# A two-layer graph attention kernel: table products of the first layer issued in fours on four PSUM banks, and the second layer's queries made inside the second layer

## The chip, the cores and the metric

The kernel runs on one core of a Trainium2 chip. The metric is device time in microseconds (us) for one launch, from the host's side of the program to its end; a profiled execution of the same program gives the span from its first to its last instruction and the time of every instruction.

## What is computed

A graph of 6250 nodes (128 features) and 200,000 edges goes through two layers of typed multi-head attention (8 heads of 16). Cut to what matters:

```python
def typed_linear(x, t, W):                 # one of 16 matrices per node, by its type
    y_all = jnp.einsum('nd,tdo->nto', x, W)
    return jnp.take_along_axis(y_all, t[:, None, None], axis=1)[:, 0]

def gt_layer(x, ntype, etype, src, dst, Wk, Wq, Wv, Wa, Watt, Wmsg, pri, skip, g, b):
    k, q, v = (typed_linear(x, ntype, W).reshape(n, 8, 16) for W in (Wk, Wq, Wv))
    kT = jnp.einsum('nhd,htdo->nhto', k, Watt)      # 32 edge types: the "table"
    vT = jnp.einsum('nhd,htdo->nhto', v, Wmsg)
    a = jnp.einsum('ehd,ehd->eh', kT[src, :, etype], q[dst]) * pri[:, etype].T / 4.0
    hag = segment_sum(vT[src, :, etype] * edge_softmax(a, dst, n)[:, :, None], dst)
    h = silu(typed_linear(hag, ntype, Wa))
    h = h * alpha + x * (1.0 - alpha)               # alpha = sigmoid(skip[ntype])
    return layernorm(h) * g + b

out = layernorm(x + (gt_layer(gt_layer(x)) @ ff_w + ff_b))
```

## The kernel before

Nodes are put in order of their degree and cut into 49 tiles of 128. A table in device memory holds, for every node and each of 32 edge types, 256 numbers (the products kT and vT). A preparation stage sorts, makes the first layer's table and lasts to about 0.8 ms. Then two layers follow one another.

In a layer GpSimd (POOL) issues 1613 gathers (`gather`, L887): each is an indirect DMA that brings one edge of each of 128 nodes from the table into a ring in SBUF (64 slots in the first layer, 96 in the second). VectorE (DVE) attends over the ring (`attend`: products at L908, sums at L910, weighting at L935, sums at L939); a tile has 61 edges at first and 23 at the end. Tiles are taken in 15 groups (`LAST`: ten of 4 tiles, then 3, 2, 2, 1, 1, numbered from 0). When a group's attention is done, `behind` applies the typed matrix Wa: transposes on TensorE (PE), 16 masks on DVE (`typed_cols`, L1010: the columns of nodes of one type), 16 matmuls on PE (L1018), then activation, skip and norm.

In the first layer `project` follows: it stores h (`hid`), runs 16 more masks and 3 x 16 matmuls with the second layer's Wk, Wv and Wq into the banks ak, av and aq, and turns the third product into rows that it stores as `qrows`. `next_tables` then makes the second layer's table, tile by tile: `table_rows` issues 16 matmuls a tile (L472) of 32 rows by 512 columns, two half-tiles of 8, which ScalarE (ACT) or DVE copy from PSUM into one of two staging buffers st (L481); `scatter` (L1130) sends each half with one indirect DMA of 2 MB issued by POOL, between the gathers. All of a group's steps in the first layer hold one lane (banks xb, aq, av; a lock), so that groups follow one another there. The first layer's own queries (`first_rows`) use the lane too. The second layer loads its queries from `qrows`. It cannot begin before the last scatter has landed, since it gathers from that table.

The order on each engine is written down by a planner (`Plan`): threads yield an engine, a duration and the times that they need; the planner takes the one that can start first (a rank breaks ties) and emits its instructions. Each engine runs its instructions in this order, whatever the real times are. A scatter is placed on POOL 8 us (`MARGIN`) after the planned end of its half's copies; in the last two groups without that margin.

In `table_rows` the number of banks decides the form, and a matmul that is planned alone is taken to use a quarter of PE:

```python
quad = rows if len(banks) >= rows else 1          # rows = 4
us = yield "PE", Work(TAB, QUAD if quad > 1 else width / P), [*needs, *emptied[-len(banks):][:quad]]
```

Of the kernel before, what the change touches and what calls it, by code (L numbers as in the profile page):

```python
# [31 lines left out]
F32 = mybir.dt.float32  # L32
# [27 lines left out]
XML = (4, 16)  # L60
# [6 lines left out]
RANK = dict(table=0, empty=0, gather=1, attend=1.6, prepare=2, mask=3, typed=3, late=4, query=1, behind=1.2, masks=1.4)  # L67
# [164 lines left out]
def gnn_kernel(ctx: ExitStack, tc: tile.TileContext, x, src, dst, etype, ntype, Wk, Wq, Wv, Wa,  # L232
# [636 lines left out]
    tabs, ak, av, aq = [bank(ps, f"tab{i}") for i in range(3)], bank(ps, "ak"), bank(ps, "av"), bank(ps, "aq")  # L869
# [13 lines left out]
    wq0 = []  # L883
# [62 lines left out]
    def query_rows(fp, n0, q):  # L946

        xo = fp.tile([P, GT, P], F32, tag="xs", name="xs", bufs=XS[0])
        nc.sync.dma_start(out=xo[:, 0], in_=xperm[ds(n0, P)])
        kinds = fp.tile([P, GT * P], F32, tag="types", name="types", bufs=XS[0])  # L950
        nc.sync.dma_start(out=kinds[:, :P], in_=tyrow[ds(n0, P)][None, :].to_broadcast([P, P]))
        nc.tensor.transpose(xb[:, :P], xo[:, 0], ident)
        for t in range(NT):
            xm = fp.tile([P, GT * P], F32, tag="xm", name="xm", bufs=XML[0])
            nc.vector.scalar_tensor_tensor(xm[:, :P], kinds[:, :P], float(t), xb[:, :P], op0=ALU.is_equal, op1=ALU.mult)
            nc.tensor.matmul(aq[:, :P], wq0[0][:, t], xm[:, :P], start=(t == 0), stop=(t == NT - 1))
        qT = fp.tile([P, GT * P], F32, tag="yT", name="yT")
        nc.vector.tensor_copy(qT[:, :P], aq[:, :P])
        nc.tensor.transpose(xb[:, :P], qT[:, :P], ident)
        nc.vector.tensor_copy(q, xb[:, :P])  # L960

    def attend_over(fp, layer, ring):
# [3 lines left out]
        with tc.For_i(0, rounds, 1):  # L966
            nc.sync.dma_start(out=over.rearrange("(t p) c -> p t c", p=P), in_=low)
            with tc.For_i(0, NP, P) as n0:
# [17 lines left out]
                if layer:  # L986
                    nc.sync.dma_start(out=q, in_=qrows[ds(n0, P)])
                else:
                    query_rows(fp, n0, q)
# [11 lines left out]
    def typed_cols(fp, xm_bufs, xT, types, M, maps, needs):  # L1001
# [11 lines left out]
        plan.spawn(mask(), RANK["masks"])  # L1013
# [43 lines left out]
    def behind(fp, layer, i, hag, fetched, needs, weights, wa, at):  # L1057
# [5 lines left out]
        xb, aq, av, lock = lane  # L1063
# [4 lines left out]
        us = yield from typed_cols(fp, XML[layer], xT, types, M, [(wa, aq)], [us, got])  # L1068
        yT, us = yield from copied4(fp, "yT", aq, M, [us], 1 + layer)
# [22 lines left out]
    def project(fp, i, h, types, weights, needs, at):  # L1092
# [44 lines left out]
    def head(fp, i, h, lane, needs, at):  # L1137
        xb, _, av, lock = lane
# [7 lines left out]
        for j in range(n):  # L1146
            nc.tensor.matmul(av[:, j * P : (j + 1) * P], oT[:, j * P : (j + 1) * P], fw, start=True, stop=True)
# [4 lines left out]
        nc.vector.tensor_tensor(o, av.rearrange("p (j m) -> p j m", j=GT)[:, :n],  # L1152
# [42 lines left out]
    def attends(fp, layer, ring, pieces, st, weights, wa, landed, freed):  # L1195
# [22 lines left out]
        def first_rows(i):  # L1218

            n = len(LAST[i])  # L1220
            turn = lanes[0][3].take()
# [3 lines left out]
            us = yield from typed_cols(fp, XML[layer], xT, types, n * P, [(wq0[0], aq)], [us])  # L1225
            qT, us = yield from copied4(fp, "yT", aq, n * P, [us])
# [5 lines left out]
            lanes[0][3].give(e[0])  # L1232
            rows[i] = q, e[0]
            asked[i].us = e[0]

        def load_rows(i):
            if layer:
                us = yield "SP", 0.4, ()
                rows[i] = load4(fp, "qr", qrows, LAST[i][0], len(LAST[i]), 2), us + 3.0
            else:  # L1240
                yield "SP", 0.0, [asked[i]]
# [7 lines left out]
        if not layer:  # L1249
            plan.spawn(first_rows(0), RANK["behind"])  # L1250
            plan.spawn(first_rows(1), RANK["behind"])
# [30 lines left out]
    for layer in range(L):  # L1282
        last = layer == L - 1
        with tc.tile_pool(name=f"wp{layer}", bufs=1) as wp, tc.tile_pool(name=f"fp{layer}", bufs=1) as fp, \
                tc.tile_pool(name=f"ring{layer}", bufs=1, side="right") as rp:
            locks = {"s": Lock()}
            lanes = [(xb, aq, av, Lock()), (xb, aq, av, Lock()), (*tabs, Lock())]
# [3 lines left out]
            if not last:  # L1291
                wq0.append(load_typed(wp, "wq0", Wq[0]))
# [141 lines left out]
```

## Time and profile before

| | us |
|---|---|
| three runs: median (lowest to highest) | 5501.67 (5501.55 to 5515.91) |
| the profiled execution's own time | 5500.28 |
| its span, first to last instruction | 5498.5 |
| first gather of the first layer | 802.1 |
| last gather of the first layer | 3138.98 |
| first gather of the second layer | 3288.00 |

The span falls into preparation, first layer, a stretch without gathers between the layers, and the second layer. In both layers the share of busy time is less telling than what POOL does from one gather to the next.

### The profile page before, as it was taken

The page shows a single profiled execution, that of the slowest core. Times are in us where ns is not written, and L with a number is a line of the kernel's source. Part 1 is how long each engine was busy: PE and PEld are TensorE (multiplying, and loading weights), DVE is VectorE, ACT ScalarE, POOL GpSimd, SP SyncE. Part 2 cuts the span into 40 slices and gives each one's busy share as a digit, 9 for nine tenths or more (in the row PEclk, how much of TensorE's full clock was granted, in tenths as well). Part 3 has the DMA queues.
Part 4 walks back from the last instruction along what each step waited for, and adds up shares of the span by engine and source line. Part 5 has one row for each costly group of instructions (what it writes and reads, how often), then busy time and mean ns, then how long its engine had stood idle before and what let it go on. Part 6 is the DMA issues. An engine that isn't in the chain of part 4 may idle for free. (4 is left out here: it accounts for less than half of the span.)

```text
span 5498.5 us, 34997 instructions
## 1 busy us (share of the span) xinstructions
PE 2728.7 (50%) x8557; PEld 1359.0 (25%) x8557; DVE 3741.5 (68%) x5254; ACT 953.7 (17%) x1840; POOL 3554.6 (65%) x3543
## 2 busy tenths in 40 slices
PE   6889962276677677878789870011011101111112
PEld 4555531032233233333334440000000000000002
DVE  5786746777678777767766624666676667767677
ACT  2233420021222222222223330000000000000001
POOL 0403317777777777777766417777777777777775
PEclk8899986577677677867778775555555555555556
DMA  7669883354645655565555443333333333333332
GB/s 248 261 250 399 353 320 103 106 168 158 222 160 170 220 195 168 189 215 198 189 169 206 172 159 107 102 110 109 99 108 108 109 100 108 108 110 108 104 109 77
DMA packets 315967, 917.37 MB, mean 167 GB/s; under 512 B 82465, under 2 KB 163613, under 8 KB 278121
## 3 DMA queue, kind: packets, MB, share of 16 engines
q0 software_dynamic: 176864, 645.82, 36.6%
q1 hardware_dynamic: 138888, 269.24, 13.4%
q8 instruction: 68, 1.11, 0.1%
q14 instruction: 147, 1.20, 0.1%
HBM read 482.08 MB, written 432.74 MB: 166 GB/s over the span
## 5 line engine op out<-in xcount | busy, mean ns | idle before, releaser
L887 POOL DMA_INDIRECT ring<-table,idx_all x3226 | 3242.7, 1005 | 1203.0 <-issue 961.3
L908 DVE TENSOR_TENSOR ring<-ring,sb 128x2048 f32<-128x2048 f32 (+13 forms) x261 | 453.8, 1739 | 783.8 <-DMA ring<-table,idx_all 773.0
L481 ACT COPY st<-tab 128x512 f32<-128x512 f32 x1207 | 651.9, 592 | 954.4 <-PE tab L472 713.3
L939 DVE TENSOR_REDUCE add<-ring 128x128 f32<-128x2048 f32 (+13 forms) x269 | 732.6, 2724 | 7.5
L472 PE MATMUL tab<-bk,kT 32*128 32x512 f32 x1568 | 612.3, 805 | 182.2 <-ACT st L481 177.4
L1010 DVE SCALAR_TENSOR_TENSOR xm<-types,xb 128x512 f32<-128x512 f32 (+3 forms) x848 | 469.8, 586 | 323.4 <-PE aq L1018 291.1
L472 PE MATMUL tab<-bv,vT 32*128 32x512 f32 x1568 | 558.7, 801 | 7.0 <-ACT st L481 6.5
L1018 PE MATMUL aq<-xm,wq 128*128 128x512 f32 (+3 forms) x960 | 453.8, 589 | 93.1 <-DVE xm L1010 93.1
L910 DVE TENSOR_REDUCE sb<-ring 128x128 f32<-128x2048 f32 (+13 forms) x269 | 473.0, 1758 | 7.1
L935 DVE TENSOR_TENSOR ring<-ring,sb 128x2048 f32<-128x2048 f32 (+13 forms) x269 | 469.4, 1745 | 0.0
L1018 PE MATMUL aq<-xm,wa 128*128 128x512 f32 (+3 forms) x736 | 332.7, 608 | 151.9 <-DVE xm L1010 151.3
L1172 ACT COPY sb<-qr 128x128 f32<-128x128 f32 x96 | 25.9, 270 | 1986.0 <-DVE sb L910 1789.5
L411 PE MATMUL xb<-ident,hag 128*128 128x128 f32 x75 | 25.4, 416 | 672.1 <-DVE hag L1278 669.3
L481 DVE COPY st<-tab 128x512 f32<-128x512 f32 x361 | 234.6, 686 | 156.9 <-PE tab L472 121.3
L439 PE MATMUL kv<-xm,wk 128*128 128x256 f32 (+1 forms) x800 | 262.9, 412 | 57.2 <-DVE xm L424 57.1
L472 PEld LDWEIGHTS tab<-bk,kT 32*128 32x128 f32 x1568 | 187.8, 225 | 399.0 <-ACT st L481 316.4
L1018 PEld LDWEIGHTS aq<-xm,wq 128*128 128x128 f32 x960 | 194.3, 219 | 332.4 <-issue 184.8
L1130 POOL DMA_INDIRECT table<-st,half x98 | 98.7, 1007 | 253.1 <-ACT st L481 213.2
L439 PE MATMUL kv<-xm,wv 128*128 128x256 f32 (+1 forms) x800 | 246.5, 391 | 0.0
L1018 PE MATMUL ak<-xm,wk 128*128 128x512 f32 (+3 forms) x480 | 226.2, 555 | 22.3 <-DVE xm L1010 22.2
L1018 PEld LDWEIGHTS aq<-xm,wa 128*128 128x128 f32 x736 | 152.2, 226 | 341.4 <-DVE xm L1010 205.4
L472 PEld LDWEIGHTS tab<-bv,vT 32*128 32x128 f32 x1568 | 189.5, 222 | 189.4 <-ACT st L481 133.3
(198 smaller groups left out, 2710.3 us busy)
## 6 DMA issues: line engine op xcount, KB each, us to landing
table<-st SPq DMA_DIRECT2D x196, 1024.0 KB
ring<-table,idx_all POOLq DMA_INDIRECT x3226, 2.8
state<-init SPq DMA_DIRECT2D x2, 3528.0 KB
state<-state SPq DMA_DIRECT2D x98, 72.0 KB
types<-tyrow SPq DMA_DIRECT2D x20, 256.0 KB
rows<-in_x_dram SPq DMA_DIRECT2D x24, 128.0 KB
types_i<-in_node_type_dram SPq DMA_DIRECT2D x24, 128.0 KB
xperm<-xg SPq DMA_DIRECT2D x12, 256.0 KB
```

The source lines that it names most:

```text
L439: nc.tensor.matmul(to, w[:, t], xm, start=False, stop=last_of)
L472: nc.tensor.matmul(tab, cT[here, nodes], blk[here, t0 : t0 + per].rearrange("p t o -> p (t o)"), start=True, stop=True)
L481: (nc.scalar.copy if e == "ACT" else nc.vector.tensor_copy)(to, tab.rearrange("p (t o) -> p t o", o=width))
L887: nc.gpsimd.indirect_dma_start(out=ring[:, place], out_offset=None, in_=tables[layer], in_offset=bass.IndirectOffsetOnAxis(ap=idx[:, s : s ...
L908: nc.vector.tensor_tensor(kk, kk, q[:, None, :].to_broadcast([P, m, P]), op=ALU.mult)
L910: nc.vector.tensor_reduce(sc[:, s0 : s0 + m], kk.rearrange("p s (h d) -> p s h d", h=H), axis=AX.X, op=ALU.add)
L935: nc.vector.tensor_tensor(vv.rearrange("p s (h d) -> p s h d", h=H), vv.rearrange("p s (h d) -> p s h d", h=H), sc[:, s0 : s0 + m, :, None ...
L939: nc.vector.tensor_reduce(add, vv.rearrange("p s c -> p c s"), axis=AX.X, op=ALU.add)
L1010: nc.vector.scalar_tensor_tensor(xm[:, :M], types[:, :M], float(t), xT[:, :M], op0=ALU.is_equal, op1=ALU.mult)
L1018: nc.tensor.matmul(to[:, :M], w[:, t], xm[:, :M], start=(t == 0), stop=(t == NT - 1))
L1130: s = nc.gpsimd.indirect_dma_start(out=tables[1].rearrange("(n t) c -> n (t c)", t=RT // 2), out_offset=bass.IndirectOffsetOnAxis(ap=half[ ...
L1172: nc.scalar.copy(q, rows[0][:, j])
```

## The change

The first layer's table products get a fourth bank, and so are issued in fours (one matmul for each 32-row strip, on four banks). The bank comes from aq: the lane's typed products, the first layer's queries and the project step now share av. `project` makes queries (Wq) only for groups 0 and 1, after keys and values are copied out; for groups 2 to 14 a new background thread of the second layer, `early_rows`, loads h and types, makes the masks and the 16 matmuls on two of the four table banks, and stores `qrows`. The second layer's mask buffers go from 16 to 8, and it loads Wq at its start. A loop for nodes of higher degree, which is skipped with this data, makes its queries itself in both layers.

```diff
-XML = (4, 16)
+XML = (4, 8)
-RANK = dict(table=0, ..., behind=1.2, masks=1.4)
+RANK = dict(table=0, ..., behind=1.2, masks=1.4, early=1.8)
-    tabs, ak, av, aq = [bank(ps, f"tab{i}") for i in range(3)], bank(ps, "ak"), bank(ps, "av"), bank(ps, "aq")
+    tabs, ak, av = [bank(ps, f"tab{i}") for i in range(4)], bank(ps, "ak"), bank(ps, "av")
...
     def project(fp, i, h, types, weights, needs, at):
...
-        end = yield from typed_cols(fp, XML[0], xT, types, M, [(wk, ak), (wv, av), (wq, aq)], [us])
-        at["ty"][i].us = end
+        end = yield from typed_cols(fp, XML[0], xT, types, M, [(wk, ak), (wv, av)], [us])
+        if i > 1:
+            at["ty"][i].us = end
...
         plan.spawn(next_tables(i, kT, vT, bk, bv, max(ks, vs), at), RANK["table"])
-        qT, us = yield from copied4(fp, "yT", aq, M, [end])
-        us = yield from turned(xb, qT, n, [us])
-        q, qs = yield from copied4(fp, "q", xb, M, [us])
-        lanes[0][3].give(qs)
-        yield "SP", 0.4, [qs]
-        nc.sync.dma_start(out=qrows[t0 * P : t0 * P + M].rearrange("(j p) d -> p j d", p=P),
-                          in_=q.rearrange("p (j d) -> p j d", d=P)[:, :n])
+        us = max(ks, vs)
+        if i < 2:
+            us = yield from typed_cols(fp, XML[0], xT, types, M, [(wq, av)], [us])
+            at["ty"][i].us = us
+            qT, us = yield from copied4(fp, "yT", av, M, [us])
+            us = yield from turned(xb, qT, n, [us])
+            q, us = yield from copied4(fp, "q", xb, M, [us])
+            got = yield "SP", 0.4, [us]
+            nc.sync.dma_start(out=qrows[t0 * P : t0 * P + M].rearrange("(j p) d -> p j d", p=P),
+                              in_=q.rearrange("p (j d) -> p j d", d=P)[:, :n])
+        lanes[0][2].give(us)
...
+        def early_rows():
+            xb, acc, _ = lanes[3]
+            free, sent = [0.0, 0.0], [0.0, 0.0]
+            for i, g in list(enumerate(LAST))[2:]:
+                n = len(g)
+                got = yield "SP", 0.9, [free[-2]]
+                xs = load4(fp, "xq", hid, g[0], n, 1)
+                types = fp.tile([P, GT * P], F32, tag="tq", name="tq", bufs=2)
+                nc.sync.dma_start(out=types[:, : n * P], in_=tyrow[...][None, :].to_broadcast([P, n * P]))
+                xT, us = yield from transposed(xb, xs, n, [got + 3.0])
+                us = yield from typed_cols(fp, XML[layer], xT, types, n * P, [(wqs[layer], acc)], [us], "early")
+                free.append(us)
+                qT, us = yield from copied4(fp, "qT", acc, n * P, [us])
+                us = yield from turned(xb, qT, n, [us])
+                q, us = yield from copied4(fp, "q", xb, n * P, [us, sent[-1]])
+                us = yield "SP", 0.4, [us]
+                nc.sync.dma_start(out=qrows[...], in_=q...)
+                sent.append(us + 2.5)
+                asked[i].us = us + 2.5
...
-            lanes = [(xb, aq, av, Lock()), (xb, aq, av, Lock()), (*tabs, Lock())]
+            lanes = [(xb, av, Lock()), (xb, av, Lock()), (*tabs[:2], Lock()), (*tabs[2:], Lock())]
...
+            wqs.append(load_typed(wp, "wq0", Wq[layer]))
```

Since the planner works with other durations, the order changes on every engine. Three places matter below.

On POOL, at the first group's scatters in the first layer (L887 is a gather, L1130 before and L1132 after is a scatter of half a tile), before:

```order
L887 DMA ring<-table_60,idx_all 128x256 x287
L1130 DMA table_61<-st_5708,half 12544x4096
L887 DMA ring<-table_60,idx_all 128x256 x4
L1130 DMA table_61<-st_5709,half 12544x4096
L887 DMA ring<-table_60,idx_all 128x256 x13
```

and now:

```order
L887 DMA ring<-table_60,idx_all 128x256 x275
L1132 DMA table_61<-st_5708,half 12544x4096
L887 DMA ring<-table_60,idx_all 128x256 x5
L1132 DMA table_61<-st_5709,half 12544x4096
L887 DMA ring<-table_60,idx_all 128x256 x12
```

The first scatter stands 12 gathers earlier than before; the distance from one tile's scatters to the next tile's hardly changes (4 and 13 gathers, now 5 and 12). Counted through the layer, a four-tile group's first scatter stood 86 to 97 gathers behind the group's own last gather and now stands 77 to 87 behind it. Nine scatters stand behind the last gather of the layer (ten before).

On PE, near the end of the first layer, where group 13 (one tile) applies Wa (`wa`) while the tables of group 12 are made (`tab`), before:

```order
L1018 MATMUL aq<-xm,wa 128x128 x3
L472 MATMUL tab_5444<-bv,vT 128x512
L1018 MATMUL aq<-xm,wa 128x128 x2
L472 MATMUL tab_5445<-bv,vT 128x512
L1018 MATMUL aq<-xm,wa 128x128
L472 MATMUL tab_5446<-bk,kT 128x512
```

and now:

```order
L411 MATMUL xb<-ident,hag 128x128
L1015 MATMUL av<-xm,wa 128x128 x10
L472 MATMUL tab_5444<-bv,vT 128x512
L472 MATMUL tab_5445<-bv,vT 128x512
L472 MATMUL tab_5446<-bv,vT 128x512
L472 MATMUL tab_5447<-bv,vT 128x512
L1015 MATMUL av<-xm,wa 128x128 x6
```

Table matmuls stood one by one among others and now stand four together.

On DVE, at the end of the attention over the layer's last tile (tile 48; L1278 before and L1304 after is its last instruction, `xm 128x128` are the masks of group 13's step with Wa), before:

```order
L942 TENSOR_TENSOR hag<-hag,add 128x128
L1276 TENSOR_SCALAR den<-den 128x8
L1277 RECIPROCAL den<-den 128x8
L1278 TENSOR_TENSOR hag<-hag,den 128x128
L1027 COPY q<-xb 128x256
L1010 SCALAR_TENSOR_TENSOR xm<-types,xb 128x128 x16
```

and now:

```order
L919 TENSOR_TENSOR sb<-sb,top 128x192
L1007 SCALAR_TENSOR_TENSOR xm<-types,xb 128x128 x14
L924 TENSOR_REDUCE den<-sb 128x8
L925 TENSOR_TENSOR state<-state,sb 128x8
L926 TENSOR_TENSOR den<-den,state 128x8
L927 TENSOR_TENSOR hag<-state,sb 128x128
L1007 SCALAR_TENSOR_TENSOR xm<-types,xb 128x128 x2
L935 TENSOR_TENSOR ring<-ring,sb 128x10x128
```

Group 13's masks stood behind the last tile's attention and now stand inside it.

## Rows read from the trace of the kernel before

**Rows 1.** The page, part 1: busy time by engine over the span.

```profile
PE 2728.7 (50%) x8557; PEld 1359.0 (25%) x8557; DVE 3741.5 (68%) x5254; ACT 953.7 (17%) x1840; POOL 3554.6 (65%) x3543
```

**Rows 2.** Stretch; its us; PE, PEld, DVE, ACT, POOL busy; PEclk; DMA; GB/s.

```profile
802.00:1200.00 398.00, 139.43 (x308) 61.92 (x308) 266.55 (x281) 25.46 (x51) 296.21 (x296) 0.64 0.44 121
1200.00:2400.00 1200.00, 875.41 (x1936) 377.10 (x1934) 882.76 (x1065) 283.13 (x542) 918.95 (x914) 0.71 0.57 191
2400.00:2815.00 415.00, 327.90 (x728) 141.92 (x728) 312.88 (x418) 103.64 (x202) 305.42 (x304) 0.71 0.58 195
2815.00:3139.00 324.00, 302.54 (x777) 137.30 (x775) 200.67 (x327) 88.76 (x173) 188.30 (x189) 0.77 0.50 175
3139.00:3288.00 149.00, 127.27 (x518) 76.64 (x518) 54.17 (x141) 53.67 (x101) 10.71 (x12) 0.77 0.38 155
3288.00:5448.00 2160.00, 255.01 (x644) 132.32 (x644) 1448.45 (x1778) 127.58 (x246) 1658.02 (x1649) 0.54 0.37 107
```

**Rows 3.** POOL's waits, 802 to 2400 us: total, times, longest.

```profile
POOL ring L887 <- DVE add L939: 12.7, 3, 12.1
POOL table L1130 <- ACT st L481: 4.1, 4, 3.2
```

**Rows 4.** POOL's waits, 2400 to 3139 us.

```profile
POOL table L1130 <- ACT st L481: 100.0, 20, 15.8
```

**Rows 5.** PE's timeline, 3204 to 3226 us: start, length, instruction, count.

```profile
3206.98 1.12 PE L472 MATMUL tab<-bk,kT 32*128 32x512 f32 x2
3208.03 0.49 PE L1018 MATMUL ak<-xm,wk 128*128 128x128 f32 x2
```

**Rows 6.** Groups of instructions by line, 815 to 3290 us.

```profile
L472 PE MATMUL tab<-bk,kT 32*128 32x512 f32 x784 | 487.5, 957 | 178.6 <-ACT st L481 177.4
L472 PE MATMUL tab<-bv,vT 32*128 32x512 f32 x784 | 419.6, 958 | 4.3 <-ACT st L481 4.2
L481 ACT COPY st<-tab 128x512 f32<-128x512 f32 x766 | 416.6, 591 | 630.7 <-PE tab L472 417.6 <-DMA table<-st,half 211.0
L1018 PE MATMUL aq<-xm,wq 128*128 128x512 f32 x640 | 350.5, 662 | 90.5 <-DVE xm L1010 90.5
```

**Rows 7.** PE's timeline in the preparation: matmuls of the first table.

```profile
180.69 2.45 PE L472 MATMUL tab<-bv,vT 32*128 32x512 f32 x8
...
500.79 1.14 PE L472 MATMUL tab<-bv,vT 32*128 32x512 f32 x8
501.86 0.70 PE L439 MATMUL kv<-xm,wk 128*128 128x256 f32 x2
```

**Rows 8.** Timeline from the layer's last gather to the next layer's first, all engines.

```profile
3138.98 1.01 POOL L887 DMA_INDIRECT ring<-table,idx_all  x1 [0.30 <-issue]
...
3177.00 0.29 DVE L1278 TENSOR_TENSOR hag<-hag,den 128x128 f32<-128x128 f32 x1
...
3199.64 0.29 DVE L1086 TENSOR_TENSOR h<-h,b 128x128 f32<-128x128 f32 x1
...
3220.18 0.39 PE L1018 MATMUL aq<-xm,wq 128*128 128x128 f32 x2
...
3226.91 0.48 PE L411 MATMUL xb<-ident,hag 128*128 128x128 f32 x1
...
3240.73 0.29 DVE L1086 TENSOR_TENSOR h<-h,b 128x128 f32<-128x128 f32 x1
...
3261.15 0.39 PE L1018 MATMUL aq<-xm,wq 128*128 128x128 f32 x2
...
3276.97 0.97 POOL L1130 DMA_INDIRECT table<-st,half  x1 [6.80 <-ACTq L966]
3288.00 1.05 POOL L887 DMA_INDIRECT ring<-table,idx_all  x1 [10.06 <-issue]
```

**Rows 9.** DVE in the second layer, 3288 to 5448 us: its waits, and masks by line.

```profile
DVE ring L908 <- DMA ring<-table,idx_all: 641.3, 76, 51.4
...
L1010 DVE SCALAR_TENSOR_TENSOR xm<-types,xb 128x512 f32<-128x512 f32 x80 | 48.2, 681 | 0.0
```

More of the change, by code (lines that the diff above doesn't have):

```diff
@@ L66 @@
 GS = 4
-RANK = dict(table=0, empty=0, gather=1, attend=1.6, prepare=2, mask=3, typed=3, late=4, query=1, behind=1.2, masks=1.4)
+RANK = dict(table=0, empty=0, gather=1, attend=1.6, prepare=2, mask=3, typed=3, late=4, query=1, behind=1.2, masks=1.4, early=1.8)
 PLAN_US = None
@@ L882, in gnn_kernel @@
     NG = len(LAST)
-    wq0 = []
+    wqs = []
     group_of = {t: i for i, g in enumerate(LAST) for t in g}
@@ L944, in attend, with query_rows @@
         return top, den
[L946 to L950, printed above, removed]
+    def query_rows(fp, layer, n0, q):
+        xo = fp.tile([P, GT, P], F32, tag="xs", name="xs", bufs=XS[layer])
+        nc.sync.dma_start(out=xo[:, 0], in_=(hid if layer else xperm)[ds(n0, P)])
+        kinds = fp.tile([P, GT * P], F32, tag="types", name="types", bufs=XS[layer])
         nc.sync.dma_start(out=kinds[:, :P], in_=tyrow[ds(n0, P)][None, :].to_broadcast([P, P]))
@@ L953, in query_rows @@
         for t in range(NT):
-            xm = fp.tile([P, GT * P], F32, tag="xm", name="xm", bufs=XML[0])
+            xm = fp.tile([P, GT * P], F32, tag="xm", name="xm", bufs=XML[layer])
             nc.vector.scalar_tensor_tensor(xm[:, :P], kinds[:, :P], float(t), xb[:, :P], op0=ALU.is_equal, op1=ALU.mult)
-            nc.tensor.matmul(aq[:, :P], wq0[0][:, t], xm[:, :P], start=(t == 0), stop=(t == NT - 1))
-        qT = fp.tile([P, GT * P], F32, tag="yT", name="yT")
-        nc.vector.tensor_copy(qT[:, :P], aq[:, :P])
+            nc.tensor.matmul(av[:, :P], wqs[layer][:, t], xm[:, :P], start=(t == 0), stop=(t == NT - 1))
+        qT = fp.tile([P, GT * P], F32, tag="yT", name="yT", bufs=1 + layer)
+        nc.vector.tensor_copy(qT[:, :P], av[:, :P])
         nc.tensor.transpose(xb[:, :P], qT[:, :P], ident)
@@ L985, in attend_over @@
                 q = bp.tile([P, P], F32, tag="qs", name="qs", bufs=1)
[L986 to L989, printed above, removed]
+                query_rows(fp, layer, n0, q)
                 for i in range(ROUND):
@@ L999, in attend_over, with typed_cols @@
             nc.vector.tensor_scalar(low[:, :, 1], low[:, :, 1], float(-ROUND), None, op0=ALU.add)
-    def typed_cols(fp, xm_bufs, xT, types, M, maps, needs):
+    def typed_cols(fp, xm_bufs, xT, types, M, maps, needs, rank="masks"):
         ready, busy = [When() for _ in range(NT)], [When() for _ in range(NT)]
@@ L1011, in mask @@
                 masks[t], ready[t].us = xm, us
-        plan.spawn(mask(), RANK["masks"])
+        plan.spawn(mask(), RANK[rank])
         for t in range(NT):
@@ L1062, in behind @@
         lane = lanes[layer * (1 + i % 2)]
-        xb, aq, av, lock = lane
+        xb, acc, lock = lane
         turn = lock.take()
@@ L1067, in behind @@
         at["hag"][i].us = us
-        us = yield from typed_cols(fp, XML[layer], xT, types, M, [(wa, aq)], [us, got])
-        yT, us = yield from copied4(fp, "yT", aq, M, [us], 1 + layer)
+        us = yield from typed_cols(fp, XML[layer], xT, types, M, [(wa, acc)], [us, got])
+        yT, us = yield from copied4(fp, "yT", acc, M, [us], 1 + layer)
         us = yield from turned(xb, yT, n, [us])
@@ L1137, in head @@
     def head(fp, i, h, lane, needs, at):
-        xb, _, av, lock = lane
+        xb, acc, lock = lane
         g = LAST[i]
@@ L1146, in head @@
         for j in range(n):
-            nc.tensor.matmul(av[:, j * P : (j + 1) * P], oT[:, j * P : (j + 1) * P], fw, start=True, stop=True)
+            nc.tensor.matmul(acc[:, j * P : (j + 1) * P], oT[:, j * P : (j + 1) * P], fw, start=True, stop=True)
         got = yield "SP", 0.4, [at["out"][i - 4]] if i > 3 else ()
@@ L1220, in first_rows @@
             n = len(LAST[i])
-            turn = lanes[0][3].take()
+            xb, acc, lock = lanes[0]
+            turn = lock.take()
             yield from load_inputs(i)
@@ L1224, in first_rows @@
             xT, us = yield from transposed(xb, xs, n, [got, turn])
-            us = yield from typed_cols(fp, XML[layer], xT, types, n * P, [(wq0[0], aq)], [us])
-            qT, us = yield from copied4(fp, "yT", aq, n * P, [us])
+            us = yield from typed_cols(fp, XML[layer], xT, types, n * P, [(wqs[0], acc)], [us])
+            qT, us = yield from copied4(fp, "yT", acc, n * P, [us])
             us = yield from turned(xb, qT, n, [us])
@@ L1247, in ask @@
                                qs, ready[t]), RANK["query"], plan.free["DVE"])
-        if not layer:
+        if layer:
+            plan.spawn(early_rows(), RANK["behind"])
+        else:
             plan.spawn(first_rows(0), RANK["behind"])
```

14 lines of the change are left out of this document (7 added, 7 removed).

## The prediction, made before the changed kernel was run

> **What bounds the kernel now.** The page gives shares over all stages [rows 1]; no engine is over 68% busy, which says little. I went on to the windows by stage [rows 2]. In the second layer POOL issues 1649 indirect DMAs in 2160 us, 1.310 us each; the busy part of one is about 1.0 us and the rest is the pitch of issue. It never waits: the second layer lasts as long as its issues take, whatever PE (255 of 2160 us busy) and DVE do. The first layer has the same 1613 gathers and 98 scatters. From its first to its last gather POOL issues 296 + 914 + 304 + 189 = 1703 in 2337 us; at 1.310 us that is 2231, so about 106 us are lost. The waits name them: 12.1 us once at the start and four short ones up to 2400 us [rows 3], then 100.0 us in 20 waits of a scatter for the copies that fill its half-tile [rows 4]. After the last gather come 149 us without a gather (3139 to 3288), in which the last tiles' tables are made.
>
> So there are two things to win: 100 us of scatters that come to POOL too early and hold the gathers behind them, and part of the 149 us.
>
> Why do the scatters wait only late? From 2815 to 3139 us PE is busy 302.5 of 324 us, 93%, against 73% between 1200 and 2400 [rows 2]; ACT, which the waits name, is busy 88.8 of 324. The tiles have fewer and fewer edges, so less time per tile, but PE's work per tile stays. PE is what the copies wait for. The planner did not see this: it counts a table matmul planned alone as a quarter of a matmul. The trace shows that one between full-width matmuls keeps PE for 1.05 us (the next starts at 3208.03 after 3206.98 [rows 5]).
>
> **The change, part by part.**
>
> *Tables in fours, first layer.* Before, 784 table matmuls keep PE 487.5 + 419.6 = 907 us [rows 6], 1.16 us each. Four on four strips and banks take 1.07 us together in the preparation (500.79 to 501.86), or 2.45 us in a slow early row, which I take as the low clock [rows 7]. 196 fours make 210 to 480 us. PE loses 427 to 697 us.
>
> *No Wq in `project` for groups 2 to 14.* A Wq matmul of 512 columns takes 350.5/320 = 1.10 us (each is two records) [rows 6]. 41 of 49 tiles are spared 16 matmuls of a quarter of this: 180 us of PE, and 17.5 us off the time for which one four-tile group holds the lane, besides two copies and the transposes.
>
> Together PE's 1773 us in the first layer become about 900 to 1170, half of its span or less, in the late stretch too. The granted clock will then sit lower: it was 0.64 when PE was 35% busy and 0.77 at 93%, and 0.54 at 12% [rows 2]. The 2.45 us above are that case, and I use the low clock as the bad end of every PE term.
>
> *The scatters' places.* The order puts a four-tile group's first scatter some ten gathers (13 us) earlier behind the group's last gather. Wq alone gives back 17.5 us of that chain, so the places are no harder to keep than in the stretch up to 2400 us, where 4.1 us were lost [rows 3]. There the planner's quarter-matmul was wrong as well, but PE had room. The fours are counted at what they take. I leave 15 us of the 100 (ends: 0, and 50 if the chain after a group is late in half of the cases). **Gain 85 (50 to 98).**
>
> Here the Trainium skill speaks against the change (TensorEngine Tiling (Array Packing), section PSUM Bottleneck): tiling speeds up TensorE but not the evacuation of PSUM, and the copy may become the bottleneck. The trace agrees that copies are a floor, 16 x 0.591 = 9.5 us a tile if ACT does them alone [rows 6]; by that rule tables would be no faster than this, and the scatters' waits, which name ACT, would stay: rival 1 below, at 5460 instead of 5375.
>
> *The stretch after the last gather* [rows 8], step by step:
> - Attention over the last tile ends at 3177.3, 38.3 us after the last gather. Kept, though group 12's `project` runs in it and is spared 16 matmuls of 256 columns, half of 1.10 us each [rows 6]: up to 9 us may go.
> - Group 13 then applies Wa and norms, to 3199.9: 22.6 us. In the new order its masks stand inside that attention, because the lane is free earlier. DVE's 16 masks must then be added to the attention; one of 128 columns takes at most half of the 0.603 us that one of 512 takes [rows 9], so 5 us. Gain 17 (0 if the lane still comes late).
> - Group 13's `project` to 3220.6: 20.7 us. After: 16 x 2 matmuls of 128 columns, a quarter of 1.10 us each [rows 6], 8.8 us at that mean clock of 0.71 and 12.5 at 0.5, and two fours of 1.07 to 2.45. Gain 8 (3 to 10).
> - To group 14's first transpose at 3226.9: 6.3 us for copies and the query's transpose, of which two copies remain. Gain 4.
> - Group 14's Wa and norm to 3241.0: 14.1 us. Kept.
> - Its `project` to 3261.4: 20.4 us. As above. Gain 8 (3 to 10).
> - Tables of the last tile to the last scatter at 3277.0: 15.6 us. Four fours with four copies each, three on ACT and one on DVE: about 4 x (1.07 + 3 x 0.591) = 11.4 us, plus hand-overs. Gain 3 (0 to 4).
> - From the last scatter to the next layer's first gather, 11.0 us: landing. Kept.
>
> **Sum of the stretch: 40 (15 to 59).** 15 is what is left when the 17 fall out and the others stand a little over their low ends; 59 is the sum of the high ends (9 + 22 + 10 + 4 + 10 + 4).
>
> *The early queries, second layer.* 208 masks, of which 128 have 512 columns at 48.2/80 = 0.603 us: 77 us, with the smaller ones at most 125; 208 matmuls, 13 loads of h and types and 13 stores. DVE waits 641.3 us for gathers in this layer [rows 9], and the ring's 96 slots hold two tiles and more once they have under 48 edges, so masks fall into those waits. PE is 12% busy. Cost 0; if nothing hid them, 125. The stores stand on SP's queue ahead of later tiles' state loads; the store waits for a copy by ACT that is planned late, so I take nothing. Mask buffers 16 to 8 and shared banks: behind the gathers, nothing. The load of the second Wq (1 MB) runs while the last tables are made: nothing.
>
> *Groups 0 and 1* make queries after their tables begin: 32 more masks, in the stretch where POOL loses nothing. The bank shared by three steps is under the same lock as before: nothing.
>
> **Sum.** The profiled execution took 5500.28 us, within 0.03% of the median of 5501.67. 5500 - 85 - 40 = **5375 us**. The sums of the ends: 5500 - 98 - 59 = 5343, 5500 - 50 - 15 = 5435.
>
> **The rivals.**
>
> 1. *Waits stay, only the stretch gets shorter.* The scatters wait for copies, as the rows name, or for staging buffers, and not for PE. For it: rows 4 name ACT, and with all four banks in one four PE and the copies can no longer overlap. Against: ACT is 27% busy where the waits are. The 100 us stay: 5500 - 40 = 5460. Chance 0.12.
> 2. *The stretch stays.* The waits go, but the chain of the last groups hangs on staging buffers and the low clock: DVE's copies for older tables now stand between the masks of the last group, and each waits for a scatter to land. 5500 - 85 = 5415, or somewhat less. Chance 0.10.
> 3. *Slower: the scatters are placed too early everywhere.* They stand 13 us earlier behind their group, at a lower clock. The ten four-tile groups have 80 scatters; if each waits 5.0 us, the mean of the twenty late ones [rows 4], POOL loses 400 us: 5500 - 40 - 98 + 400 = 5764. It decides from 1.9 us a scatter on (138 + 16 us over 80). Against: Wq's 17.5 us. Chance 0.05.
> 4. *Given back in the second layer.* The masks hold up attention until the ring is full: up to 125 us, which is all of the gain: 5500. Against: 641 us of waiting. Chance 0.03.
>
> **How the numbers follow.** The forecast, waits gone and stretch shorter, has 0.70, with 5343 to 5410 as its own range. 5340 to 5440 takes in rival 2 and the ends of the terms, and leaves out rivals 1, 3, 4: 0.20. About 0.3% (16 us) is what a measurement of this kernel can tell from no change. Faster by more: forecast and rivals 1 and 2, 0.92. Within: rival 4, 0.03. Slower: rival 3, 0.05.
>
> **What would show it.** Right: POOL's waits of scatters between 2400 us and the last gather fall from 100 to under 50 us; the last gather starts near 3054 and the second layer's first near 3163, some 109 us later; from there to the end nothing changes (2210 us); PE is under 70% busy in the last 300 us before the last gather. Wrong: scatters that wait in the early groups (rival 3), gathers of the second layer that wait for the ring (rival 4), or an unchanged distance from last to first gather (rival 2). The least certain term is the 17 us of overlap in the stretch between the layers.

## The result, and the profile after

| | before | after |
|---|---|---|
| median (lowest to highest), us | 5501.61 (5490.6 to 5515.91), 4 runs | 5362.03 (5360.09 to 5362.46), 4 runs |
| ratio, 95% interval | | 0.9744 [0.9722, 0.9767] |
| span of the profiled execution | 5498.5 | 5360.0 |
| last gather of the first layer | 3138.98 | 3043.32 |
| from there to the second layer's first gather | 149.0 | 104.5 |
| from there to the end | 2210.5 | 2212.2 |

The change made the kernel 2.6% faster; the forecast was 5375. The span's 138.5 us are 95.7 us before the last gather and 44.5 us between the layers, less 1.7 us behind. Part 1 of the page and the windows by stage (columns as in [rows 1, 2]; the fourth ends at the last gather, the fifth is the stretch between the layers):

```profile
PE 2562.4 (48%) x8598; PEld 1357.9 (25%) x8598; DVE 3876.2 (72%) x5522; ACT 919.8 (17%) x1814; POOL 3552.9 (66%) x3543
```

```profile
802.80:1200.00 397.20, 137.72 (x336) 61.03 (x336) 275.45 (x296) 32.13 (x64) 295.55 (x295) 0.65 0.44 125
1200.00:2400.00 1200.00, 703.09 (x1754) 333.56 (x1754) 908.93 (x1107) 255.46 (x506) 920.21 (x916) 0.68 0.57 190
2400.00:2743.00 343.00, 215.67 (x585) 105.25 (x586) 269.42 (x349) 88.00 (x179) 263.48 (x262) 0.71 0.61 208
2743.00:3043.30 300.30, 229.68 (x768) 127.84 (x768) 249.76 (x420) 95.76 (x196) 230.56 (x229) 0.79 0.65 225
3043.30:3147.80 104.50, 67.75 (x364) 47.20 (x362) 46.84 (x119) 36.54 (x71) 9.76 (x10) 0.76 0.53 208
3147.80:5308.00 2160.20, 506.81 (x1113) 250.62 (x1114) 1545.86 (x1979) 137.79 (x271) 1657.67 (x1650) 0.59 0.38 111
```

In the last 300 us before the last gather PE is busy 229.7 of 300.3 us, 76%, where it was 93% [rows 2]; POOL runs at its pitch of 1.31 us there (229 issues in 300 us; before, 189 in 324). POOL's waits of scatters, 803 to 3020 us, answer to [rows 3, 4]:

```profile
POOL table L1132 <- issue: 21.3, 70, 0.3
POOL table L1132 <- ACT st L481: 5.2, 17, 0.3
POOL table L1132 <- DMA ring<-table,idx_all: 0.3, 1, 0.3
```

No scatter waits for anything: 0.3 us is the idle time between any two issues, and none of the 88 is above it. The stretch between the layers, from the timelines (start, length, engine, line, [idle before <- releaser]), which answers to [rows 8]:

```profile
3043.32 1.00 POOL L887 DMA_INDIRECT ring<-table,idx_all  x1 [0.30 <-issue]
...
3069.78 0.29 DVE L1304 TENSOR_TENSOR hag<-hag,den 128x128 f32<-128x128 f32 x1
3070.89 0.29 DVE L1083 TENSOR_TENSOR h<-h,b 128x128 f32<-128x128 f32 x1
...
3083.14 0.39 PE L1015 MATMUL av<-xm,wv 128*128 128x128 f32 x2
...
3087.28 0.33 PE L411 MATMUL xb<-ident,hag 128*128 128x128 f32 x1
...
3102.84 0.29 DVE L1083 TENSOR_TENSOR h<-h,b 128x128 f32<-128x128 f32 x1
...
3115.28 0.39 PE L1015 MATMUL av<-xm,wv 128*128 128x128 f32 x2
...
3120.74 0.97 POOL L1132 DMA_INDIRECT table<-st,half  x1 [8.24 <-ACT st L481]
...
3129.14 0.97 POOL L1132 DMA_INDIRECT table<-st,half  x1 [7.44 <-DMA table<-st,half]
3136.38 0.73 SPq L305 DMA_DIRECT2D wq<-in_L_gnn_Wq_dram  x1
3137.57 1.47 SPq L305 DMA_DIRECT2D wa<-in_L_gnn_Wa_dram  x1
...
3147.81 1.06 POOL L887 DMA_INDIRECT ring<-table,idx_all  x1 [17.71 <-issue]
```

| step (ends) | before | after | gain | forecast |
|---|---|---|---|---|
| attention of the last tile (L1304) | 38.3 | 26.7 | 11.6 | 0, up to 9 |
| group 13's Wa and norm (L1083) | 22.6 | 1.1 | 21.5 | 17 |
| group 13's project (last Wv matmul) | 20.7 | 12.4 | 8.3 | 8 |
| to group 14's first transpose (L411) | 6.3 | 3.8 | 2.5 | 4 |
| group 14's Wa and norm | 14.1 | 15.9 | -1.8 | 0 |
| group 14's project | 20.5 | 12.5 | 8.0 | 8 |
| to the last scatter | 15.4 | 13.5 | 2.0 | 3 |
| to the next layer's first gather | 11.0 | 18.7 | -7.7 | 0 |

Two rows stand out: attention became shorter, and the last step longer. For the first, DVE's waits between 802 us and the last gather, of the kernel before and then of the kernel after:

```profile
DVE xm L1010 <- PE aq L1018: 253.8, 281, 4.6
```

```profile
DVE xm L1007 <- PE av L1015: 80.6, 216, 2.4
```

A mask waits until PE has used an older one, and the attention's operations stand behind it on DVE. Over the layer this costs a third of what it did. In the attention over the last tile itself (before: 3138.98 to 3177.3 us, after: 3043.32 to 3070.1), before and then after:

```profile
DVE xm L1010 <- PE aq L1018: 6.8, 7, 1.8
```

```profile
DVE xm L1007 <- PE av L1015: 0.8, 1, 0.8
```

DVE's idle time in this step fell by 4.2 us (7.7 to 3.5; these waits by 6.0, but a wait of 1.6 for a gather is new), and its busy time by 7.3 (30.6 to 23.3). Before, DVE still had to finish the tile before the last one when the last gather was issued; that took it until 3145.9. That earlier mask waits had put it behind is likely, but not shown. For the last step, SP's waits from 3130 to 3150 us:

```profile
SPq L305 <- DMA table<-st,half: 7.7, 1, 7.7
SPq L966 <- DMA wa<-in_L_gnn_Wa_dram: 3.4, 1, 3.4
SPq L966 <- DMA wq<-in_L_gnn_Wq_dram: 2.6, 1, 2.6
```

The second Wq is not loaded while the last tables are made: SP issues it only when the last scatter has landed, and the branch of the loop for nodes of higher degree (L966), which all engines pass before the second layer, waits for it. The rows name the load of Wa as well; the kernel with Wq kept, below, tells the two apart. Before, the first gather (3288.00 [rows 8]) started 1.5 us behind the issue of Wa:

```profile
3286.49 0.75 SPq L305 DMA_DIRECT2D wa<-in_L_gnn_Wa_dram  x1
```

### The profile page after: what moved, and what is told of

Its sections match the earlier page's. It is cut to its first block, busy times and chain, and to the rows that moved or that the text cites. A ratio compares the mean times of both kernels' runs of the same rounds, so it can differ in the third digit from the quotient of the medians.

```text
span 5360.0 us, 35414 instructions
## 1 busy us (share of the span) xinstructions
PE 2562.4 (48%) x8598; PEld 1357.9 (25%) x8598; DVE 3876.2 (72%) x5522; ACT 919.8 (17%) x1814; POOL 3552.9 (66%) x3543
## 5 line engine op out<-in xcount | busy, mean ns | idle before, releaser
L887 POOL DMA_INDIRECT ring<-table,idx_all x3226 | 3240.8, 1005 | 1211.3 <-issue 970.0
L481 ACT COPY st<-tab 128x512 f32<-128x512 f32 x1175 | 614.2, 598 | 860.4 <-PE tab L472 437.7
L1007 DVE SCALAR_TENSOR_TENSOR xm<-types,xb 128x512 f32<-128x512 f32 (+3 forms) x880 | 485.6, 588 | 103.5 <-PE av L1015 91.3
L472 PE MATMUL tab<-bv,vT 32*128 32x512 f32 x1568 | 405.1, 781 | 305.6 <-ACT st L481 303.9
L1015 PE MATMUL tab<-xm,wq 128*128 128x512 f32 (+3 forms) x416 | 215.6, 686 | 465.8 <-DVE xm L1007 465.8
L1015 PE MATMUL av<-xm,wa 128*128 128x512 f32 (+3 forms) x736 | 329.1, 610 | 201.5 <-DVE xm L1007 201.1
L472 PE MATMUL tab<-bk,kT 32*128 32x512 f32 x1568 | 380.7, 780 | 25.4 <-ACT st L481 11.5
L1015 PE MATMUL av<-xm,wq 128*128 128x512 f32 (+3 forms) x544 | 237.2, 589 | 128.4 <-DVE xm L1007 126.3
L472 PEld LDWEIGHTS tab<-bv,vT 32*128 32x128 f32 x1568 | 174.2, 219 | 451.0 <-ACT st L481 401.6
L1015 PEld LDWEIGHTS av<-xm,wa 128*128 128x128 f32 x736 | 156.5, 230 | 369.2 <-DVE xm L1007 244.0
L1015 PEld LDWEIGHTS tab<-xm,wq 128*128 128x128 f32 x416 | 101.1, 269 | 568.3 <-DVE xm L1007 508.1
L1015 PE MATMUL av<-xm,wv 128*128 128x512 f32 (+3 forms) x480 | 222.0, 546 | 0.0
L1015 PE MATMUL tab<-xm,wa 128*128 128x512 f32 (+2 forms) x224 | 114.1, 672 | 178.6 <-DVE xm L1007 178.6
```

The costliest lines, as they stand in the source:

```text
L472: nc.tensor.matmul(tab, cT[here, nodes], blk[here, t0 : t0 + per].rearrange("p t o -> p (t o)"), start=True, stop=True)
L481: (nc.scalar.copy if e == "ACT" else nc.vector.tensor_copy)(to, tab.rearrange("p (t o) -> p t o", o=width))
L887: nc.gpsimd.indirect_dma_start(out=ring[:, place], out_offset=None, in_=tables[layer], in_offset=bass.IndirectOffsetOnAxis(ap=idx[:, s : s ...
```

## The experiments

My theory: PE was full with single table matmuls, and the planner did not know it. The scatters' waits are the part of this delay that falls before the last gather, and the stretch between the layers the part behind it. Rivals: the length of a group's chain (Wq and the lane), the planner's price alone, and the copies out of PSUM. Each kernel ran beside the kernel before, whose median was 5510.2 us for the first four, 5506.5 for the next four and 5507.4 for the last two; the intervals are 7 to 16 us to either side. The kernel before alone thus differs by 9 us between sessions (5501.6 beside the changed kernel), so that differences of a few us between medians of different sessions tell nothing by themselves; there the traces decide. The columns behind the ratio are from one profiled execution of each kernel.

| kernel | median us | ratio to before [95%] | scatter waits | last gather | between the layers | both |
|---|---|---|---|---|---|---|
| before | 5501.6 | | 104 | 3139.0 | 149.0 | 253 |
| after | 5362.0 | 0.9744 [0.9722, 0.9767] | 0 | 3043.3 | 104.5 | 105 |
| fours alone | 5385.5 | 0.9780 [0.9751, 0.9810] | 0 | 3036.8 | 136.6 | 137 |
| moved queries alone | 5461.3 | 0.9925 [0.9905, 0.9945] | 87 | 3122.9 | 147.0 | 234 |
| price alone | 5476.6 | 0.9941 [0.9922, 0.9960] | 7 | 3049.3 | 220.7 | 228 |
| moved queries and price | 5430.3 | 0.9858 [0.9829, 0.9887] | 0 | 3041.0 | 181.8 | 182 |
| Wq kept | 5345.3 | 0.9702 [0.9689, 0.9715] | 0 | 3044.2 | 91.3 | 91 |
| early queries twice | 5394.9 | 0.9795 [0.9781, 0.9808] | 0 | 3042.5 | 104.2 | 104 |
| fours, Wq kept | 5381.2 | 0.9767 [0.9754, 0.9781] | 0 | 3044.6 | 128.9 | 129 |
| Wq kept, unchained | 5345.7 | 0.9705 [0.9691, 0.9719] | 0 | 3042.7 | 90.0 | 90 |
| copies twice | 5407.2 | 0.9818 [0.9802, 0.9835] | 0 | 3036.5 | 158.6 | 159 |
| no margin | 5377.0 | 0.9766 [0.9749, 0.9783] | 23 | 3064.2 | 100.6 | 124 |

(Scatter waits are the sum of POOL's idle times over 0.5 us before scatters up to the last gather.)

**Fours alone.** All groups' queries in the first layer again:

```diff
-        if i < 2:
+        if True:
             us = yield from typed_cols(fp, XML[0], xT, types, M, [(wq, av)], [us])
...
-            plan.spawn(early_rows(), RANK["behind"])
```

> The changed kernel with all fifteen groups' queries made in the first layer again (Wq after keys and values are copied, as it does for groups 0 and 1); the table products stay in fours. The planned places of the scatters are within a few gathers those of the changed kernel. My theory: the scatters waited because PE was full with single table matmuls that were planned at a quarter of what they take. Then the fours alone free most of it: waits of scatters before the last gather under 30 us, last gather at 3045 to 3075, no second weight load between the layers, so 105 to 120 us from there to the second layer's first gather, and 5360 to 5405 us in all (5385). Rival, the lane: Wq's matmuls made the chain of a group late; then 60 us or more of waits stay and the time is 5430 or more.

Measured 5385.5, no scatter waits, and the last gather at 3037, before the expected 3045. The lane rival is out. In the kernel before the same scatters stood up to 20 gathers later and waited all the same, so it is not their places. The stretch between the layers is 137 us, above the expected 105 to 120: this kernel too loads the second Wq there (18.8 us from the last scatter to the first gather), and the last tile's two scatters start 22.9 us behind the ones before them.

**Moved queries alone.** The banks that decide the form:

```diff
-            halves = yield from table_rows(tabs, at["rows"], kT, vT, j, bk, bv, [us, turn], free)
+            halves = yield from table_rows(tabs[:3], at["rows"], kT, vT, j, bk, bv, [us, turn], free)
```

> The changed kernel with table matmuls issued one by one on three of the four banks, planned at a quarter of a matmul as in the kernel before; queries of groups 2 to 14 in the second layer. The order of scatters among the gathers is the changed kernel's. My theory: PE is still full with singles of 1.05 us; it is spared Wq only, so 50 to 110 us of scatter waits stay before the last gather, 120 to 140 us between the layers, 5440 to 5500 us in all (5465). Rival, the lane: without Wq the chain is 17.5 us shorter and the waits are under 20 us: 5365 to 5390.

Measured 5461.3. The scatters stand within 8 gathers of their places in the changed kernel (those of groups 9 to 11 stand 2 to 6 earlier, which may make a part of their waits), and wait (POOL, 803 to 3020 us):

```profile
POOL table L1132 <- ACT st L481: 74.7, 17, 14.9
```

The profiled execution took 5479.8 us, 18 above the median of its nine runs; the median run has probably less of these waits than the 87 us of the table.

**Price alone.** In the kernel before:

```diff
-                    us = yield "PE", Work(TAB, QUAD if quad > 1 else width / P), [...]
+                    us = yield "PE", Work(TAB, QUAD if quad > 1 else 1.0), [...]
```

> The kernel before with one number changed: a table matmul issued alone is planned as a whole matmul instead of a quarter. Same instructions, other order: the late groups' scatters stand up to some twenty gathers later, and 15 instead of 12 of them are planned behind the last gathers. My theory: waits of scatters fall from 100 to under 40 us, but PE has as much to do, so what is not waited for before the last gather comes after it: 155 to 180 us between the layers, 5430 to 5480 us in all (5455). Rival, the price is everything: waits gone and the stretch between the layers no longer than before, 5400 or less. Rival, capacity alone: waits stay near 100 us, 5490 or more.

Measured 5476.6: the waits are gone but for one of 6.8 us, and 72 us of them came back behind the last gather, more than I expected (220.7 us between the layers for 155 to 180). The windows before and behind the last gather:

```profile
2743.00:3049.30 306.30, 273.19 (x696) 136.44 (x695) 222.40 (x339) 98.71 (x193) 232.72 (x232) 0.73 0.64 221
3049.30:3270.00 220.70, 180.15 (x715) 125.39 (x714) 83.47 (x196) 69.43 (x134) 13.62 (x14) 0.74 0.33 138
```

PE is still 89% busy before the last gather, and has 180 us left to do behind it. An honest price decides where the delay shows and takes little of it away: 253 us in both columns of the table became 228.

**Moved queries and price.** The two edits above in one.

> Single table matmuls on three banks, planned as whole matmuls, and the queries of groups 2 to 14 in the second layer: the changed kernel without its fours but with a price near to what singles take. My theory: the honest price removes most of the waits (under 40 us), PE's load keeps the stretch between the layers at 115 to 140 us: 5385 to 5430 us (5405), so that the fours themselves are worth 25 to 65 us. Rival, the price is everything: 5362 within 12 us, the fours are worth nothing by themselves.

Measured 5430.3, the upper end. Its scatters stand up to 18 gathers later than the changed kernel's, three more of them stand behind the last gather, and the stretch is 181.8 us for 104.5: the fours themselves are worth 68 us (5430 - 5362; 63 by the ratios) where queries are moved and the price is honest. The fours come with a fourth bank, and singles on four banks were not run; what the bank alone does is open.

**Wq kept.** The second Wq goes once, at the start, into a pool that outlives both layers (the first layer's `project` uses the same tile):

```diff
+    wq1 = bp.tile([P, NT, P], F32, tag="wq1", name="wq1", bufs=1)
+    nc.sync.dma_start(out=wq1, in_=Wq[1].rearrange("t d o -> d t o"))
...
-            wqs.append(load_typed(wp, "wq0", Wq[layer]))
+            if not last:
+                wqs += [load_typed(wp, "wq0", Wq[0]), wq1]
```

> The changed kernel, but the second layer's Wq is loaded once, at the start, into memory that outlives both layers; no weights of Wq are loaded between the layers. My theory: the loop for nodes of higher degree uses this tile, so the second layer's first gather waited for the 1 MB that could be fetched only when the last scatter had landed. Then the last scatter to the first gather takes 11.0 us as in the kernel before instead of 18.7, nothing else changes, and the time falls by 8 us to 5354 (5350 to 5357). Rival: the load of Wa, which is fetched at the same moment, holds the gather as well; then 16 us or more remain and the time is 5359 to 5364.

Measured 5345.3, 17 us less instead of 8 (23 by the ratios). The end of the stretch:

```profile
3124.76 0.96 POOL L1133 DMA_INDIRECT table<-st,half  x1 [7.44 <-DMA table<-st,half]
3134.30 0.74 SPq L305 DMA_DIRECT2D wa<-in_L_gnn_Wa_dram  x1
...
3135.50 1.05 POOL L888 DMA_INDIRECT ring<-table,idx_all  x1 [9.77 <-issue]
```

10.7 us for 18.7: the load of Wq cost the 8 us, and Wa's costs nothing. The rest is not the load's. From last gather to last scatter it takes 80.6 us for 85.8, in steps in which PE was granted more clock. Group 13's project and the stretch to group 14's, after and then with Wq kept:

```profile
3070.30:3083.30 13.00, 11.68 (x73) 10.52 (x73) 5.75 (x20) 2.98 (x6) 0.34 (x1) 0.71 0.35 142
3083.30:3104.30 21.00, 15.33 (x74) 9.30 (x76) 9.84 (x34) 9.73 (x18) 2.27 (x3) 0.78 0.49 204
```

```profile
3071.20:3082.70 11.50, 10.22 (x72) 9.05 (x73) 5.71 (x20) 2.95 (x6) 0.26 (x1) 0.80 0.37 153
3082.70:3100.30 17.60, 12.84 (x74) 7.11 (x77) 8.86 (x31) 9.73 (x18) 1.87 (x3) 0.89 0.57 240
```

The same instructions, in the same order on every engine, take 1.5 and 3.4 us less at 0.80 and 0.89 than at 0.71 and 0.78. And the second layer's gathers take 2152.9 us for 2157.6, a length that kernels with the load have too (2153.0 with the fours alone). A first gather 4.9 us later and a first layer 4.0 us shorter nearly cancel. Why the clock was higher here no run settles; that it makes the steps shorter is argued from these two windows alone.

**Early queries twice.** `early_rows` runs over each group two times.

> The changed kernel with each group's background queries of the second layer made and stored twice (the same values): another 208 masks, some 125 us of DVE, 13 loads and 13 stores. My theory: they fall into DVE's waits for gathers (537 us in the changed kernel), and the second layer lasts 2212 us, or up to 6 us longer: 5362 to 5368. Rival: a part of the first set was paid for at the layer's start, where the ring is filled by tiles of many edges; then the second set costs 15 to 60 us: 5377 to 5420.

Measured 5394.9: 33 us more. My expectation failed, and the rival was right in size and wrong in place. The masks of `early_rows` in the kernel after, and then with two sets (count, least, median and longest ns, first and last start; the shapes are counted in a sample):

```profile
L1007 DVE SCALAR_TENSOR_TENSOR xm<-tq,tab x208: 277/678/684, 3175.0 to 4840.8; 128x512 f32<-128x512 f32 x64, 128x256 f32<-128x256 f32 x16, 128x128 f32<-128x128 f32 x16, 128x384 f32<-128x384 f32 x8
```

```profile
L1007 DVE SCALAR_TENSOR_TENSOR xm<-tq,tab x416: 253/679/689, 3173.9 to 5381.9; 128x512 f32<-128x512 f32 x86, 128x256 f32<-128x256 f32 x22, 128x128 f32<-128x128 f32 x21, 128x384 f32<-128x384 f32 x10
```

One set is done at 4841 us, 465 us before the last gather at 5305. Two sets go on to 5382, past the last gather (5325 there). DVE's waits for gathers from 5000 us to the end, in the kernel after and then with two sets:

```profile
DVE ring L908 <- DMA ring<-table,idx_all: 66.1, 14, 11.2
```

```profile
DVE ring L908 <- DMA ring<-table,idx_all: 2.3, 2, 1.9
```

With two sets DVE has no reserve left in the last 300 us: gathers take 2177.9 us from first to last for 2157.6, and from the last one to the end it takes 73 us for 55. At the 1400th gather of the layer the kernel with two sets is still 4 us ahead (1870 us from the first for 1874), so the layer's start costs nothing with one set or two.

**Fours, Wq kept.** The first edit and that of Wq kept.

> The fours alone (all queries made in the first layer) and the second layer's Wq loaded once at the start, so that no weights of Wq are loaded between the layers. With the same change on both sides, the difference to the changed kernel with Wq kept is what the moved queries are worth. My theory: 8 us less than the fours alone (5385.5), 5378 (5373 to 5382), and 20 to 28 us above the changed kernel with Wq kept. Rival, the boundary is set by something else: 5383 to 5388.

Measured 5381.2. The boundary fell from 18.8 to 10.7 us, as in the other pair; the median by 4 only. In the profile the first gather stands 5.1 us later (806.6 for 801.5), which I leave open: profiles of other kernels here, one without this edit among them, start at 807 as well. Wq kept in both, the moved queries are worth 36 us, more than the 20 to 28 expected; some 5 of them go with the clock above.

**Wq kept, unchained.** A line in `scatter` that makes it forget the scatter before it (`on_pool[0] = None`).

> The changed kernel with the second layer's Wq kept, and without the dependence that makes a scatter wait for the scatter before it to land where no gather stands between them (behind the last gather; they write rows of different nodes). In the changed kernel the last scatter starts 5.4 us after its copies for that reason. My theory: two scatters then share the DMA engines, which move some 290 GB/s in either case, so of the 5.4 us only the hand-over comes back: 1 to 3 us less than with the dependence, 5351 to 5354. Rival: the engines had room; 4 to 6 us less. Rival: sharing is slower or nothing changes: 0 to 2 us more.

Measured 5345.7, no difference in the medians; in the traces the stretch is 1.3 us shorter, as expected. The last scatter starts 4.3 us earlier behind the last gather (76.3 for 80.6) and needs 13.7 us for 10.7 to the first gather, which fits transfers that share the DMA engines.

**Copies twice.**

```diff
-                            done.us, e = yield ("ACT", "DVE"), (act_us(TAB), dve_us(TAB)), [us, free[i]]
+                            for k in range(times):
+                                at, e = yield ("ACT", "DVE"), (act_us(TAB), dve_us(TAB)), [us, free[i]]
```

> The changed kernel with each of the first layer's 784 table copies out of PSUM made twice in a row (the same values, planned twice): some 463 us of copies more at 0.59 us each, on ACT and DVE. My theory: copies were not what the scatters waited for, and with ACT at 21% and the fours off the path there is room; the planner puts the scatters some ten to twenty gathers later, 14 instead of 10 behind the last gathers, so only the stretch between the layers grows, by 10 to 30 us: 5370 to 5392 us, no more than 15 us of scatter waits. Rival, the copies out of PSUM set the pace once the products are fast: waits of 50 us and more come back and the time is 5415 or more.

Measured 5407.2: no scatter waits and the last gather no later, but 158.6 us between the layers. That is outside the range of my theory and short of the rival's 5415. The planner knew of the doubled copies and placed the scatters up to 28 gathers later, so the run does not say what they would cost at the changed kernel's places: doubled copies need not hold the gathers, but on the chain behind the last gather they cost 54 us, nearly twice the most that I allowed.

**No margin.** `MARGIN` is 0 in all groups.

> The changed kernel with scatters planned at the end of their copies, without the 8 us of margin, in every group: a group's first scatter stands up to 5 and its last up to 23 gathers earlier. In the changed kernel half of the scatters start 14 us or more after their half is filled, and the tightest 2.7 us. My theory: places too early cost what they fall short, so few wait and only by some us: 5 to 25 us of waits before the last gather, the stretch between the layers as before, 5365 to 5390 us. Rival, the changed kernel's order has no reserve (the slower case of the prediction): 50 us of waits or more, 5410 or above. Rival, nothing waits: 5362 within 4 us.

Measured 5377.0; 9 scatters wait 23.2 us in all, the longest 4.7, and the last gather is 21 us later. The rival that there is no reserve is out: in the order as it ran scatters stand up to 20 gathers earlier (a few up to 5 later), and it costs a quarter of a microsecond a scatter.

## Why the prediction was right

*Waits of the scatters (85, measured 95.7).* Right in mechanism: the last gather at 3043 for the forecast 3054. I had left 15 us of waits; none stayed. Price alone and moved queries alone show that it takes PE's relief: without the fours most of the same delay (228 and 234 of 253 us) is either waited for or worked off behind the last gather.

*PE's relief was mis-sized.* Groups of instructions of the kernel after, 815 to 3130 us (answers to [rows 6]):

```profile
L472 PE MATMUL tab<-bv,vT 32*128 32x512 f32 x784 | 267.1, 919 | 302.5 <-ACT st L481 301.5 <-DVE st L481 0.9
L472 PE MATMUL tab<-bk,kT 32*128 32x512 f32 x784 | 255.6, 907 | 21.8 <-ACT st L481 11.5 <-DVE st L481 8.4 <-ACT kT L1022 1.6
L1015 PE MATMUL av<-xm,wq 128*128 128x512 f32 x384 | 196.1, 666 | 109.8 <-DVE xm L1007 109.8
```

The two rows of table products overlap in time, here and in [rows 6], so their busy times may not be added. All table matmuls together (L472), of the kernel before and then of the kernel after (stretch; its us; PE, PEld busy; PEclk; DMA; GB/s):

```profile
815.00:3290.00 2475.00, 717.26 (x1568) 284.69 (x1568) 0.71 0.53 176
```

```profile
815.00:3147.80 2332.80, 480.10 (x1568) 245.71 (x1568) 0.70 0.56 186
```

The step of the prediction that failed here is "784 table matmuls keep PE 907 us": it is 717. The 196 fours keep PE 480 us, 2.45 each, my upper end. So the fours relieve PE by 237 us, where I said 427 to 697, and the typed matmuls by 188 (180 forecast). The windows of the first layer and the stretch behind it add to 1354 us of PE for 1773: a relief of 419, where the prediction had 607 to 877, and PE was 76% busy where I said under 70%. Nor did the granted clock sit lower (0.70 for 0.71). That so much less relief was enough is luck of the forecast.

The upper end itself rests on a second misreading: I took the 2.45 us in [rows 7] as the low clock. The window of that row (columns as in [rows 2]) shows a granted clock of 1.00, 2.4 GHz:

```profile
180.69:183.14 2.45, 2.45 (x13) 0.85 (x8) 1.92 (x5) 2.26 (x5) 1.84 (x3) 1.00 1.00 402
```

The four matmuls of that four begin 0.4 to 0.5 us apart, and so do ACT's copies that empty the banks: the row priced the copies, not the clock. In the kernel after, two fours at the low level (granted 0.50, 1.2 GHz), the first waiting bank by bank for copies and the second with its four matmuls begun at once:

```profile
2373.21 3.54 PE L472 MATMUL tab<-bv,vT 32*128 32x512 f32 x8 [4.37 <-ACT st L481]
...
2377.73 2.09 PE L472 MATMUL tab<-bk,kT 32*128 32x512 f32 x8
```

PE's time in the first layer and the stretch behind it also goes with the column "both": 1354 us in the kernel after, 1443 with the fours alone, 1590 with moved queries and price, 1667 with moved queries alone, 1728 with the price alone, 1773 before. Only moved queries alone and price alone stand the other way round there (234 and 228).

*The stretch between the layers (40, measured 44.5)* came out in its sum by two errors that nearly cancel. Attention, "kept", gave 11.6, in part since DVE's masks wait less for PE; the load of the second Wq, "while the last tables are made: nothing", cost 7.7. This last step failed: memory of the first layer's pools is free only when their last scatter has landed. The 17 us of overlap, the term that I trusted least, came as 21.5. (Two slips in the sums: by its row in [rows 8] group 14's project ends at 3261.5, not 3261.4, and rival 3 adds up to 5762, not 5764.)

*Rival 1 and the copies.* By the Trainium skill (TensorEngine Tiling (Array Packing), PSUM Bottleneck) the copies may become the limit once tiling makes TensorE fast. Here that holds in place, not for the kernel: PE idles 302 us for ACT's copies ahead of the fours (179 before [rows 6]), and behind the last gather doubled copies cost 54 us, but no scatter waits. Rival 1 itself is out: the waits went from 104 us to none with the same 784 copies.

*Rival 3* is priced by the kernel without margin: 15 us slower than the changed kernel by the medians, which the two intervals (0.9766 and 0.9744) do not tell from nothing, and 23.2 us in POOL's waits. *Rival 4 and the second layer (0, measured +1.7):* right for one set of early queries, but the cover that I named was not as wide as it looked. 641 us of DVE's waits [rows 9] did not take a second 125 us without loss. The waits are spread over the layer, and a second set used up those at its end. What counts is when the thread is done.

## What to carry to other kernels

A delay that shows as waits on one engine's queue can be moved behind the end of a stage by a better order and hardly get smaller (253 us to 228 here); add the waits and the stage's tail, and see which resource is full in both. Cost a weight load at a stage's boundary as on the path until the trace shows that its memory is free earlier: here, loading it once took the last step from 18.7 to 10.7 us. For background work, compare the time at which it ends with the time at which its last result is needed, not with the sum of idle time.

## What was not expected of the hardware

Identical instructions between the layers took 85.8 us in one kernel and 80.6 us in another, with granted clocks of 0.71 to 0.78 and 0.80 to 0.89 in the same steps. Two scatters of half a tile at once need nearly as long as one behind the other: they start 8.4 us apart when chained and 3.8 when not, and the next layer's first gather comes only 1.3 us earlier. A four of table matmuls took 1.07 us in the preparation with its banks empty, and 2.45 us at a granted clock of 1.00 where copies emptied its banks one by one.
